# Place columns turned in the second graph layer, seven gathered pairs in flight there, inputs on two queues, and a reordered start

## The chip, the cores and the metric

The kernel runs on one core of one Trainium2 chip. The metric is the device time of one execution in microseconds (us), the median of several runs. PE is the matrix engine, DVE the vector engine, ACT the scalar engine, POOL the GpSimd engine and SP the engine that here only issues DMAs.

## The reference

Two graph layers on 6250 nodes of 128 numbers and 106250 edges, sorted by their destination `dst`:

```python
h = relu(layernorm(x))
x = x + L0(h, src, dst, edge_type)          # attention over 4 edge types
h = relu(layernorm(x))
x = x + L1(h, edge_attr, src, dst)          # two-layer network on every edge, and on every node

# L0, for each of the 4 relations, 8 heads of 16 numbers
xr = h @ W;  logit = leaky_relu(es[src] + ed[dst], 0.2)      # es, ed: xr with a_src, a_dst
alpha = softmax of logit over the edges of one dst and one type
out = segment_sum(alpha * xr[src], dst) + b
# then the 4 outputs (gelu, @ W_cross) and h @ W_self are weighed by a softmax over these 5

# L1: an edge (s, d) is used in both directions
edge_in = [nf[src_full], nf[dst_full], ef_full]              # 128 + 128 + 64
msg = leaky_relu(edge_in @ We1) @ We2
red = segment_sum(msg, dst_full)
return leaky_relu([nf, red] @ Wn1) @ Wn2
```

## The kernel before

**Tiles.** Nodes are cut into NU = 50 tiles of 126, each into two blocks of 63 (NBK = 100 blocks). Since edges are sorted by destination, a block's edges are one stretch of at most 9 × 128 = 1152 edges (TB = 9 tiles, CAP edges), whose first edge is read from a small table on the chip (`st0`) at run time. An edge that doesn't belong to the block is masked by `inb`.

**Start (L190–L433).** SP loads `src`, `dst`, `et`; ACT's queue issues the loads of x in ten-tile blocks (L220, L222), then the weights and the attention vectors (L230–L241). DVE works out where blocks start, and SP writes and reloads `e2`, the edges' source rows and destinations, by block (`ct`, L347: 100 DMAs). The table loop (L353–L378) runs over the 50 tiles: every ten tiles the layernorm and relu of ten (`layernorm_relu`, L145–L152: sums on DVE, the Square L148 on ACT), then for each tile a transpose L358, matmuls L365, the copy L366 into `row`, an own row with x and the bias `blb` (L373, stored by ACT L374) and two stores of `row` to the table `xt` on POOL's queue (L377). Behind the loop, ten groups of `ct` are turned from rows into columns (L384–L393: a cast, two transposes, a copy into `xi`, a subtraction into `dloc`), and `srci`, `inb` and `key` are worked out from these (L395–L402).

**Layer 0 (L438–L859).** NS = 25 steps of four blocks (Q = 4), nine tiles each. POOL's gathers (L81, from `xt` by `xi`) run LA0 = 17 tiles ahead in a ring of 18 tiles `xg`. The edge work of step s + 1 is woven by the written order into step s: `masks`, `logits` (L521), the scans of `soft` (L552–L570), which make the softmax, `turn` (L577), then in step s + 1 itself `messages` (L584, L591, L592); `nodes` of the step before (L621–L705) is handed out in pieces within `messages`, and ends with stores to `abtab`, layer 1's table. `loads(s)` (L498 and around) brings sixteen DMAs of lane data on SP's queue. For the second layer, DVE counts how many edges have their source in each of the 50 tiles (`count`, L721, in steps 0 to 3 by the written order), ranks them (`rank`, L763–L766), and writes every edge's place to `plcd`. In steps 20 to 24 `place_load` (L774–L778) reads these places back by block, ten DMAs a group into one of three buffers `ctp`, and `place_turn` (L781–L789) turns them into columns `placei`: one transpose, three DVE operations.

**Layer 1 (L914–L1076).** 450 pairs of tiles. `gather_pair(n + 3)` (two L81 gathers from `abtab` into one of five buffers `ag`), matmuls L1046, the sum L1048, the leaky relu L1049 and L1050, the source column L1051 into `s` (four buffers), two scatters L1054 of s by `placei` into `m2d`, and the sums over the destination L1064. `ready(u + 1)` (L987–L1021) prepares the next tile: loads of `fe`, `db` and rows of `abtab` on SP, transposes L1013. `windows(j)` (L935–L966) sums the scattered rows by source, once the scatters of one of five parts are issued: loads `mt` on SP (L943), L959, the one-hot L963, matmuls L964. `node_update` (L872–L908) ends the kernel together with the last part's windows.

**What sets the order.** Every engine runs its instructions in one order, which a scheduler makes from the program's order, the data's ties and the buffers. An instruction passed to `keep_in_program_order` isn't moved against its neighbours. DMAs are issued by the engine named, in that engine's order; POOL issues all gathers and scatters.

Of the kernel before, what the change touches and what calls it, by code (L numbers as in the profile page):

```python
# [21 lines left out]
P = 128  # L22
# [4 lines left out]
R = 4  # L27
# [29 lines left out]
LA0 = 17  # L57
NCS = 4
# [18 lines left out]
AHEAD = 3  # L77
# [8 lines left out]
def kernel(ctx: ExitStack, tc: tile.TileContext, x, src, dst, ef, et, w_rel, a_src, a_dst,  # L86
# [106 lines left out]
    with ExitStack() as prep:  # L193
# [4 lines left out]

        ints = {}
# [13 lines left out]
        for u0 in range(0, NU, 10):  # L213
            nc.gpsimd.memset(x_sb[:, u0:u0 + 10, :], 0.0)
            for q in range(2):
                n0 = u0 * DB + q * GB
                k = 10 if u0 + 10 < NU else 9
                xq = x[u0 * DB:(u0 + k) * DB, :].rearrange("(u q r) c -> q r u c", q=2, r=GB)[q]
                for r0, r1 in ((0, 48), (48, GB)):
                    nc.scalar.dma_start(x_sb[q * 64 + r0:q * 64 + r1, u0:u0 + k, :], xq[r0:r1])  # L220
        for h, n in halves(NU - 1):
            nc.scalar.dma_start(x_sb[h, NU - 1, :], x[n, :])  # L222


        wall = cpool.tile([P, R * XR + R * H + C + 2 * H], F32, name="wall")
        wx = wall[:, 0:R * XR].rearrange("p (r c) -> p r c", r=R)
        wd = wall[:, R * XR:R * XR + R * H].rearrange("p (r h) -> p r h", r=R)
        wso = wall[:, R * XR + R * H:]
        wr = cpool.tile([P, R, C], F32, name="wr")
        nc.scalar.dma_start(wr, w_rel.rearrange("r i o -> i r o"))  # L230
        nc.scalar.dma_start(wso[:, 0:C], w_self)
        nc.scalar.dma_start(wcx[:, 0:C], w_cross)
        nc.scalar.dma_start(brT, b_rel.rearrange("r c -> c r"))
        blb = cpool.tile([P, C], F32, name="blb")
        nc.scalar.dma_start(blb, b_l.partition_broadcast(P))
        tmp = cpool.tile([P, R * C], F32, name="tmp")

        def scores(o, w, a, r):

            ab = wpool.tile([P, R * C], F32, name="ab")  # L240
            nc.scalar.dma_start(ab[:, 0:r * C], a.partition_broadcast(P))  # L241
            tt(tmp[:, 0:r * C].rearrange("p (r c) -> p r c", r=r), w,
               ab[:, 0:r * C].rearrange("p (r c) -> p r c", r=r), op=ALU.mult)
            red(o, tmp[:, 0:r * C].rearrange("p (r h d) -> p r h d", r=r, d=D), axis=AX.X, op=ALU.add)

        nc.gpsimd.tensor_copy(wx[:, :, 0:C], wr)
        scores(wx[:, :, C:XR], wr, a_src.rearrange("r h d -> (r h d)"), R)
        scores(wd, wr, a_dst.rearrange("r h d -> (r h d)"), R)
        ws1 = wso[:, 0:C].rearrange("p (r c) -> p r c", r=1)
        scores(wso[:, C:C + H].unsqueeze(1), ws1, a_src_l.rearrange("h d -> (h d)"), 1)  # L250
        scores(wso[:, C + H:C + 2 * H].unsqueeze(1), ws1, a_dst_l.rearrange("h d -> (h d)"), 1)
        wc1 = wcx[:, 0:C].rearrange("p (r c) -> p r c", r=1)
        scores(wcx[:, C:C + H].unsqueeze(1), wc1, a_src_l.rearrange("h d -> (h d)"), 1)
# [97 lines left out]

        for u in range(NU):
            if u % 10 == 0:  # L353
# [9 lines left out]
            w = R * XR // 2  # L363
            for k in range(2):
                nc.tensor.matmul(ps[:, k, 0:w], hT, wall[:, k * w:(k + 1) * w], start=True, stop=True)  # L365
            nc.vector.tensor_copy(row.rearrange("p (a c) -> p a c", a=2), ps[:, :, 0:w])  # L366
# [12 lines left out]


        first = cpool.tile([P, NBK, TB], F32, name="first")
        nc.gpsimd.iota(first, [[GB, NBK], [0, TB]], base=0, channel_multiplier=0, allow_small_or_imprecise_dtypes=True)
        w = CG * TB
        for g in range(NBK // CG):  # L384
            ct = cts[g]
            ctf = wpool.tile([w, 2, P], F32, name="ctf")
            nc.vector.tensor_copy(ctf, ct)
            tp = pp.tile([P, 2, w], F32, name="tp")
            for a in range(2):
                nc.tensor.transpose(tp[:, a, :], ctf[:, a, :], ident[0:w, 0:w])  # L390
            s = slice(g * w, (g + 1) * w)
            nc.vector.tensor_copy(xi[:, s], tp[:, 0, :])
            tt(dloc[:, s], tp[:, 1, :], first.rearrange("p b i -> p (b i)")[:, s], op=ALU.subtract)  # L393
        ti = cpool.tile([P, NT], I32, name="ti")
        ts_(ti, xi, R - 1, None, op0=ALU.bitwise_and)  # L395
        ts_(srci, xi, 2, None, op0=ALU.logical_shift_right)
        nc.vector.tensor_copy(srcf, srci)
        ts_(inb, dloc, 0.0, None, op0=ALU.is_ge)
        stt(inb, dloc, float(GB), inb, op0=ALU.is_lt, op1=ALU.mult)
        stt(key, ti, 64.0, dloc, op0=ALU.mult, op1=ALU.add)  # L400
        stt(key, key, 1.0, inb, op0=ALU.add, op1=ALU.mult)
        ts_(key, key, -1.0, None, op0=ALU.add)  # L402
# [35 lines left out]
    with ExitStack() as s1_:  # L438
# [38 lines left out]
        xgs, lanes, pes = {}, {}, {}  # L477

# [142 lines left out]
        def nodes(s, g, gt, last):  # L621
# [20 lines left out]
            tt(va, gt[:, :, 0:R].rearrange("p v t -> p t v"), gt[:, :, 1:R + 1].rearrange("p v t -> p t v"), op=ALU.is_gt)  # L642
# [64 lines left out]
        def node_turns(s, done):  # L707

            if done:
                yield from nodes(s - 1, *done, s == NS)  # L710
            yield
            g = (s - NS) * 3 + NBK // CG
            for k in range(3):
                if 0 <= g + k < NBK // CG:
                    place_turn(g + k)
                    yield

        def count(b):

            ind = wp.tile([P, J], U8, name="ind", bufs=1)  # L720
            ts_(ind, skey, float(b), None, op0=ALU.is_equal, op1=ALU.add, accum_out=cnt[:, b:b + 1])  # L721
# [38 lines left out]
        def rank(b):  # L760
# [7 lines left out]

        trash = cp.tile([P, CG * TB], F32, name="trash")
        nc.gpsimd.iota(trash, [[0, 2], [P, CG * TB // 2]], base=E, channel_multiplier=1,  # L770
                       allow_small_or_imprecise_dtypes=True)
        pcs = {}

        def place_load(g):  # L774
            ct = wp.tile([CG * TB, P], F32, name="ctp", bufs=3)
            regs = first_of(st0, g * CG, CG, E - CAP)
            for k in range(CG):
                nc.sync.dma_start(ct[k * TB:(k + 1) * TB], plcd[0, ds(regs[k], CAP)].rearrange("(i p) -> i p", p=P))  # L778
            pcs[g] = ct

        def place_turn(g):  # L781
            w = CG * TB
            s = slice(g * w, (g + 1) * w)
            tp = pa.tile([P, 512], F32, name="ent")
            nc.tensor.transpose(tp[:, 0:w], pcs.pop(g), ident[0:w, 0:w])
            pf = wp.tile([P, w], F32, name="pf", bufs=1)
            tt(pf, tp[:, 0:w], trash, op=ALU.subtract)
            tt(pf, pf, inb[:, s], op=ALU.mult)
            tt(placei[:, s], pf, trash, op=ALU.add)  # L789

# [8 lines left out]

        masks(0)  # L800
# [11 lines left out]
        for s in range(NS):  # L812
# [7 lines left out]
            for i in range(TB):  # L820
# [15 lines left out]
                if s < NCS:  # L836
                    for b in range(s * TB + i, NU, NCS * TB):
                        count(b)
# [8 lines left out]
                g = (s - NS + 1) * 3 + NBK // CG + (i - 3) // 2  # L847
                if 0 <= g < NBK // CG and i in (3, 5, 7):
                    place_load(g)
# [812 lines left out]
```

## Time and profile before

| what | value |
|---|---|
| runs shown | 4169.11, 4176.27, 4177.46 us; median 4176.27 |
| the profiled execution | 4172.47 us, span of the instructions 4170.7 us |
| granted PE clock | 0.86 (mean) |
| busy | PE 3111.7, DVE 2830.8, POOL 2899.4, ACT 1574.8 us |
| memory traffic | 754.26 MB, 180 GB/s |
| POOL's first store of a row to `xt` | 60.73 us |
| POOL's first gather in layer 0 | 164.16 us |
| POOL's first instruction of layer 1 | 1556.43 us |

The page's second part shows the span in 40 slices of 104 us, a digit for the tenths that an engine was busy. Its DMA row and GB/s row are those of the transfers:

```profile
DVE  6767899999777744455556665566657666577755
ACT  2356666656666532222222332222222222222211
DMA  6645444445555417666578886788868888588754
GB/s 180 168 102 120 113 113 114 114 112 119 118 119 122 105 41 202 175 180 184 165 212 247 252 253 197 227 249 240 246 197 265 242 237 251 170 263 274 242 164 139
```

Slices 1 and 2 are the start, 2 to 14 are layer 0, slice 15 with its 41 GB/s is the passage to layer 1, slices 16 to 38 are layer 1, and the last two the end. The busy time of an indirect DMA on POOL is the time in which its descriptors are made; the transfer itself runs behind it on the DMA engines. A group's idle time that ends by "issue" waited for nothing that the profile shows.

### The profile page before, as it was taken

Reading aid. Unit: us, or ns where it says so; the run is one execution under the profiler, and the core shown is the slowest. Engines: PE = TensorE matmul, PEld = TensorE weight load, DVE = VectorE, ACT = ScalarE, POOL = GpSimd, SP = SyncE. Lnnn points to the kernel's source line nnn. Section 1 sums busy time; section 2 is a strip of 40 time slices with the busy share of each in tenths; the row PEclk is TensorE's granted clock in tenths of the full one; section 3 lists DMA queues with packets and bytes.
Section 4 is the critical chain, followed back from the end, with each engine's and each line's share of the span. In section 5 each row is a group of like instructions: output and inputs, shape, how many; then the busy total and the mean of one; then the engine's idle time right before and its main releaser. Section 6 shows DMA issues by size and latency. Waiting matters only on the chain. (4 is left out here: it accounts for less than half of the span.)

```text
span 4170.7 us, 43560 instructions
## 1 busy us (share of the span) xinstructions
PE 3111.7 (75%) x11258; PEld 1790.3 (43%) x11258; DVE 2830.8 (68%) x5244; ACT 1574.8 (38%) x2994; POOL 2899.4 (70%) x2887
## 2 busy tenths in 40 slices
PE   4558877777888855666678887688768787688888
PEld 3346555555666642222234443344324333244456
DVE  6767899999777744455556665566657666577755
ACT  2356666656666532222222332222222222222211
POOL 5777777777777506777777777777777777777700
PEclk9768878888888868788889898888989989899999
DMA  6645444445555417666578886788868888588754
GB/s 180 168 102 120 113 113 114 114 112 119 118 119 122 105 41 202 175 180 184 165 212 247 252 253 197 227 249 240 246 197 265 242 237 251 170 263 274 242 164 139
DMA packets 414703, 754.26 MB, mean 181 GB/s; under 512 B 182863, under 2 KB 249525, under 8 KB 414445
## 3 DMA queue, kind: packets, MB, share of 16 engines
q0 software_dynamic: 148800, 430.91, 35.6%
q1 hardware_dynamic: 230376, 288.41, 26.6%
q10 hardware_dynamic: 35268, 32.07, 2.7%
q8 instruction: 92, 1.51, 0.2%
q14 instruction: 167, 1.36, 0.1%
HBM read 586.43 MB, written 164.69 MB: 180 GB/s over the span
## 5 line engine op out<-in xcount | busy, mean ns | idle before, releaser
L81 POOL DMA_INDIRECT xg<-xt,xi x900 | 980.5, 1089 | 289.0 <-issue 237.8
L81 POOL DMA_INDIRECT ag<-abtab,srci x900 | 907.4, 1008 | 303.4 <-issue 203.0
L1054 POOL DMA_INDIRECT m2d<-s,placei x900 | 913.9, 1015 | 288.6 <-issue 213.7
L1046 PE MATMUL z<-rhs,lt 128*128 128x512 f32 x1800 | 1037.5, 703 | 0.6 <-ACT lt L1017 0.6
L1050 DVE TENSOR_TENSOR s<-s,z 128x1024 f32<-128x1024 f32 x450 | 548.3, 1220 | 560.9 <-ACT z L1049 559.1
L1064 PE MATMUL sums<-s,oh 128*64 128x256 f32 x1800 | 338.3, 459 | 486.5 <-DVE s L1050 485.5
L1048 DVE TENSOR_TENSOR s<-z,ag 128x1024 f32<-128x1024 f32 x450 | 549.5, 1221 | 189.5 <-PE z L1046 156.0
L1049 ACT ACTIVATE z<-s 128x1024 f32<-128x1024 f32 x450 | 461.0, 1024 | 389.1 <-DVE s L1048 388.6
L592 PE MATMUL acc<-oh,msg 128*128 128x256 f32 x1800 | 501.9, 421 | 71.1 <-DVE oh L591 51.4
L1046 PEld LDWEIGHTS z<-rhs,lt 128*128 128x128 f32 x1800 | 353.2, 216 | 449.3 <-issue 442.8
L1051 ACT COPY s<-srcf 128x2 f32<-128x2 f32 x450 | 86.9, 193 | 1207.4 <-DMA m2d<-s,placei 1193.4
L964 PE MATMUL sums<-mt,ohw 128*128 128x256 f32 x2024 | 528.1, 394 | 9.2 <-DVE ohw L963 9.2
L964 PEld LDWEIGHTS sums<-mt,ohw 128*128 128x128 f32 x2024 | 392.4, 200 | 202.8 <-issue 133.9
L592 PEld LDWEIGHTS acc<-oh,msg 128*128 128x128 f32 x1800 | 363.3, 212 | 164.3 <-DVE oh L591 74.0
L1064 PEld LDWEIGHTS sums<-s,oh 128*64 128x64 f32 x1800 | 98.8, 149 | 729.7 <-DVE s L1050 570.5
L591 DVE TENSOR_SCALAR oh<-iota,key 128x256 f32<-128x256 f32 x900 | 309.6, 365 | 93.0 <-PE acc L592 88.7
L599 ACT ACTIVATE junk<-dt,nthr 128x1152 bf16<-128x1152 f32 x250 | 313.8, 1255 | 17.2 <-DMA dt<-dtyp 12.3
L963 DVE TENSOR_SCALAR ohw<-col,at 128x128 f32<-128x128 f32 x1012 | 250.5, 299 | 19.5 <-PE sums L964 11.3
L584 DVE TENSOR_TENSOR msg<-xg,pt 128x512 f32<-128x512 f32 x225 | 148.6, 676 | 86.5 <-PE pt L577 81.3
L1013 PE MATMUL tp<-ident,fe 128*128 128x128 f32 x450 | 86.6, 299 | 138.1 <-ACT lt L1017 107.2
L1017 ACT COPY lt<-tp 64x384 f32<-64x384 f32 x300 | 141.7, 472 | 111.3 <-PE tp L1013 62.7
L1013 PEld LDWEIGHTS tp<-ident,fe 128*128 128x128 f32 x450 | 58.9, 151 | 212.3 <-ACT lt L1017 140.8
(276 smaller groups left out, 3467.0 us busy)
## 6 DMA issues: line engine op xcount, KB each, us to landing
mt<-m2d SPq DMA_DIRECT2D x156, 514.0 KB
db<-in_dst_dram SPq DMA_DIRECT2D x200, 288.0 KB
mt<-m2d SPq DMA_DIRECT2D x53, 642.5 KB
dt<-dtyp SPq DMA_DIRECT2D x100, 288.0 KB
fe<-in_edge_attr_dram SPq DMA_DIRECT2D x100, 288.0 KB
mt<-m2d SPq DMA_DIRECT2D x41, 385.5 KB
xg<-xt,xi POOLq DMA_INDIRECT x900
ag<-abtab,srci POOLq DMA_INDIRECT x900
```

What stands on the lines that cost most here:

```text
L81: nc.gpsimd.indirect_dma_start(out=o, out_offset=None, in_=table, in_offset=bass.IndirectOffsetOnAxis(ap=idx.bitcast(I32), axis=0))
L591: ts_(oh.rearrange("p t n -> p (t n)"), iota, key[:, k:k + 1], None, op0=ALU.is_equal)
L592: nc.tensor.matmul(acc[q // 2][:, :, q % 2, :], msg[:, q, :], oh, start=(i == 0 and q % 2 == 0), stop=(i == TB - 1), skip_group_check=True)
L599: nc.scalar.activation(junk, lanes[s]["dt"][v], AF.Sign, bias=nthr[:, u, t:t + 1], accum_out=g[:, v, t:t + 1])
L963: ts_(oh, col, at[:, i:i + 1], None, op0=ALU.is_equal)
L964: nc.tensor.matmul(sums, oh, mt[:, i, 0:HID], start=(i == 0), stop=(i == n - 1))
L1046: nc.tensor.matmul(z[:, q, :], lt[q][:, i * P:(i + 1) * P], rhs[(2 * u + q) % 4], start=True, stop=True)
L1048: tt(s[:, :, 0:2 * HID], z, ags.pop(n), op=ALU.add)
L1049: nc.scalar.mul(z, s[:, :, 0:2 * HID], 0.01)
L1050: tt(s[:, :, 0:2 * HID], s[:, :, 0:2 * HID], z, op=ALU.max)
L1054: st = nc.gpsimd.indirect_dma_start(out=m2d, out_offset=bass.IndirectOffsetOnAxis(ap=placei[:, k:k + 1], axis=0), in_=s[:, q, HID:HID + MW ...
L1064: nc.tensor.matmul(sums[q * 64:(q + 1) * 64, :], oh[:, q * TB + i, :], s[:, q, 0:HID], start=(i == 0), stop=(i == TB - 1))
```

## The change

1. `AHEAD` becomes 7: a pair is gathered seven pairs ahead, and `ag` has nine buffers in place of five.
2. `place_load` and `place_turn` leave layer 0. A generator `places` in layer 1 does the same for one group: ten loads into a single buffer `ctp`, and the turn in the bank of PSUM that `ready` uses. Group 0 is done before the first tile, groups 1 to 9 in tiles 2, 7, ..., 42: loads at the tile's second pair, the turn at its last.
3. The weights, attention vectors (each into a buffer of its own, `ab0` to `ab3`, read once) and `blb` are loaded at the head of ACT's queue; of x, only the first two blocks stay there, the others and the last tile go to SP's queue.
4. The columns are turned in the last ten passes of the table loop, a group in each (`columns`), instead of behind it; the integer and key work L395–L402 goes into layer 0's opening, with `ti` in the memory of `key`.
5. 28 counts (`NC0`) stand ahead of the first step's masks, and the other 22 one per tile of the steps 0 to 2, pinned to the program's order, as is one operation `va` of `nodes` (L642).

The built kernel has, in its order on each engine, 18 DMAs on ACT's queue ahead of the first Square (29 before), ten place loads on SP ahead of the first `fe`, and 18 gathers on POOL (ten before) ahead of the first wait for an L1048.

```diff
+NC0 = 28
...
-AHEAD = 3
+AHEAD = 7
...
+        nc.scalar.dma_start(wr, w_rel.rearrange("r i o -> i r o"))
+        nc.scalar.dma_start(wso[:, 0:C], w_self)
+        nc.scalar.dma_start(wcx[:, 0:C], w_cross)
+        atts = []
+        for a in (a_src.rearrange("r h d -> (r h d)"), a_dst.rearrange("r h d -> (r h d)"),
+                  a_src_l.rearrange("h d -> (h d)"), a_dst_l.rearrange("h d -> (h d)")):
+            ab = cpool.tile([P, a.shape[0]], F32, name=f"ab{len(atts)}")
+            nc.scalar.dma_start(ab, a.partition_broadcast(P))
+            atts.append(ab)
+        blb = cpool.tile([P, C], F32, name="blb")
+        nc.scalar.dma_start(blb, b_l.partition_broadcast(P))
...
-                    nc.scalar.dma_start(x_sb[q * 64 + r0:q * 64 + r1, u0:u0 + k, :], xq[r0:r1])
+                    (nc.scalar if u0 < 20 else nc.sync).dma_start(x_sb[q * 64 + r0:q * 64 + r1, u0:u0 + k, :], xq[r0:r1])
         for h, n in halves(NU - 1):
-            nc.scalar.dma_start(x_sb[h, NU - 1, :], x[n, :])
+            nc.sync.dma_start(x_sb[h, NU - 1, :], x[n, :])
...
+        def columns(g):
+            ct = cts[g]
+            ctf = wpool.tile([w, 2, P], F32, name="ctf")
+            nc.vector.tensor_copy(ctf, ct)
+            tp = pp.tile([P, 2, w], F32, name="tp")
+            for a in range(2):
+                nc.tensor.transpose(tp[:, a, :], ctf[:, a, :], ident[0:w, 0:w])
+            s = slice(g * w, (g + 1) * w)
+            nc.vector.tensor_copy(xi[:, s], tp[:, 0, :])
+            tt(dloc[:, s], tp[:, 1, :], first.rearrange("p b i -> p (b i)")[:, s], op=ALU.subtract)
...
         for u in range(NU):
+            if u >= NU - NBK // CG:
+                columns(u - NU + NBK // CG)
...
+        ti = key.bitcast(I32)
+        ts_(ti, xi, R - 1, None, op0=ALU.bitwise_and)
+        ts_(srci, xi, 2, None, op0=ALU.logical_shift_right)
+        nc.vector.tensor_copy(srcf, srci)
+        ts_(inb, dloc, 0.0, None, op0=ALU.is_ge)
+        stt(inb, dloc, float(GB), inb, op0=ALU.is_lt, op1=ALU.mult)
+        stt(key, ti, 64.0, dloc, op0=ALU.mult, op1=ALU.add)
+        stt(key, key, 1.0, inb, op0=ALU.add, op1=ALU.mult)
+        ts_(key, key, -1.0, None, op0=ALU.add)
...
+            tc.keep_in_program_order(c)
...
+        for b in range(NC0):
+            count(b)
         masks(0)
...
                 if s < NCS:
-                    for b in range(s * TB + i, NU, NCS * TB):
-                        count(b)
+                    b = NC0 + s * TB + i
+                    if b < NU:
+                        count(b, True)
...
-                g = (s - NS + 1) * 3 + NBK // CG + (i - 3) // 2
-                if 0 <= g < NBK // CG and i in (3, 5, 7):
-                    place_load(g)
...
+        def places(pool, bank, g):
+
+            w = CG * TB
+            s = slice(g * w, (g + 1) * w)
+            ct = pool.tile([w, P], F32, name="ctp", bufs=1)
+            regs = first_of(st0, g * CG, CG, E - CAP)
+            for k in range(CG):
+                nc.sync.dma_start(ct[k * TB:(k + 1) * TB], plcd[0, ds(regs[k], CAP)].rearrange("(i p) -> i p", p=P))
+            yield
+            tp = bank()[:, 0:w]
+            nc.tensor.transpose(tp, ct, ident[0:w, 0:w])
+            pf = pool.tile([P, w], F32, name="pf", bufs=1)
+            tt(pf, tp, trash, op=ALU.subtract)
+            tt(pf, pf, inb[:, s], op=ALU.mult)
+            tt(placei[:, s], pf, trash, op=ALU.add)
...
+            for _ in places(wp, bank, 0):
+                pass
             for _ in ready(0):
                 pass
...
+                more = u % 5 == 2 and 2 * u + 6 < NBK
+                plcs = places(wp, bank, (2 * u + 6) // CG) if more else iter(())
...
+                    if i in (1, TB - 1):
+                        next(plcs, None)
```

## The prediction, made before the changed kernel was run

> **What bounds the kernel now.** First the page's busy shares and its 40 slices, then the groups by line, then the waits of POOL, last the timeline around POOL's idle stretches. Columns of the groups: count, busy us in all, mean ns, idle just before them and what ended most of it; of the waits: us in all, times, longest; of the timeline: start, duration, instruction, and in brackets its wait.
> ```profile
> POOL 5777777777777506777777777777777777777700
> L81 POOL DMA_INDIRECT xg<-xt,xi x900 | 980.5, 1089 | 289.0 <-issue 237.8
> L81 POOL DMA_INDIRECT ag<-abtab,srci x900 | 907.4, 1008 | 303.4 <-issue 203.0
> L1054 POOL DMA_INDIRECT m2d<-s,placei x900 | 913.9, 1015 | 288.6 <-issue 213.7
> ```
> POOL is level at 7 in every slice of both layers, and its idle time before indirect DMAs ends mostly by "issue": it waits for nobody. Layer 0 is 900 gathers from 164.16 to about 1433 (1.41 each), layer 1 is 1800 DMAs from 1556 to 3967 (1.34 each). What the change can win lies where POOL stands still: the start (to 164), the gap between the layers, and the waits within layer 1.
> ```profile
> POOL iota L919 <- DMA abtab<-at: 123.1, 1, 123.1
> POOL iota L445 <- DVE key L400: 8.2, 1, 8.2
> POOL ag L81 <- DVE s L1048: 42.8, 50, 14.1
> POOL m2d L1054 <- DVE s L1050: 18.4, 34, 2.4
> ```
> The gap is 123.1 us; the start ends with 8.2 on the keys; the 84 waits in layer 1 come to 61.2, of which 84 × 0.30 = 25 is the gap that every issue has, and 13.8 the first fill: about 22 to 25 us are real.
>
> **A. Start of the table loop.** POOL's stores of xt set the loop's pace (77.8 busy of the 95 us from 60 to 155), so an earlier first tile moves all.
> ```profile
> 26.11 1.48 DVE L147 TENSOR_TENSOR h_sb<-x_sb,ln_st 128x1280 f32<-128x1280 f32 x1
> 10.56 30.17 ACTq L220 DMA_DIRECT2D x_sb<-in_x_dram  x16
> 47.86 1.27 ACT L148 ACTIVATE sq<-h_sb 128x1280 f32<-128x1280 f32 x1
> 54.92 1.48 DVE L152 SCALAR_TENSOR_TENSOR h_sb<-h_sb,ln_st 128x1280 f32<-128x1280 f32 x1
> ```
> The Square's operand is done at 27.59; it runs at 47.86, behind the 29 DMAs that ACT issues to 46.56. The first h_sb is done at 56.40, 8.54 after the Square starts. Changed, 18 DMAs precede the Square. By shares: 8 x loads at 30.17/16 = 1.89 is 15.1, ten small ones at 0.45 is 4.5, from 8.3: 28, then a table load of 1.28: Square from 29, h_sb at 38 (−18). By the mean of all 29 ((46.56 − 8.26)/29 = 1.32, 18 × 1.32 = 24): Square at 33.6, h_sb at 42.2 (−14). Weights now land beside the first x blocks, so I go a little below the second: **−13** [−20.3, the whole wait 47.86 − 27.59, to 0]. The store of own needs blb, which landed at 48.9; it is now the eighth DMA on the queue, so it can't take the wait over.
>
> The DMA engines' share was 1.12 and 0.85 from 10 to 30 us, 0.65 and 0.49 from 30 to 50: by these rows the wait is one of ACT's instruction order, not of DMA bandwidth.
>
> The Trainium skill, "DMA: Bandwidth & Descriptors", section "Issuing engines are not separate DMA queues", speaks against this part: DMAs issued from several engines share the same 16 engines, and only the sequencers' time is saved. By that rule alone the loads of x on a second queue bring nothing and the sum would be about 13 smaller in size, −19; the rule says nothing of a compute instruction that stands behind the issues, which is what the row at 47.86 shows.
>
> **B. End of the loop to the first gather.**
> ```profile
> 152.42 1.16 POOL L377 DMA_DIRECT2D xt<-row  x2 [1.29 <-DVE row L366]
> 161.72 0.35 POOL L445 IOTA iota<- 128x256 f32 x1 [8.15 <-DVE key L400]
> 164.16 1.05 POOL L81 DMA_INDIRECT xg<-xt,xi  x1 [0.25 <-issue]
> ```
> The last store is issued at 153.58; ten column groups and the keys lie behind it, and POOL waits 8.15. Now each group (cast, two transposes, copy, subtract; DVE's share 0.29 + about 0.6) lies in one of the last ten passes, where DVE is 60 of 100 busy and POOL sets the pace; the keys go behind the pool's opening beside gathers. Removed: **−7** [−8.15 to 0, if the pool's opening still waits for another DVE instruction]. Added: columns in ten passes, **+3** [0 to 10 × 0.5 = +5, half of DVE's part showing]; keys beside gathers, **+2** [0 to +4]: DVE operations with two SBUF inputs stretch a POOL DMA from 0.95 to 1.2–1.35 (L556 1.35, L654 1.23), and there are six instructions of about 1 us. A to B: −15.
>
> **Counts.** All 50 ran from 166.6 to 221.3 (1.07 each) ahead of the first scan. With 28 ahead and 22 pinned into steps 0 to 2 the scan can come up to 22 × 1.07 = 23.5 us earlier. POOL doesn't wait there: its ring of 18 tiles is never empty of buffers before 1433. **0**; in the steps 7 or 8 counts each are covered by DVE's 29 idle of 100 us (300 to 400). Without this cover: +23.5.
>
> **C. End of layer 0.**
> ```profile
> 1423.72 11.78 SPq L778 DMA_DIRECT2D ctp<-plcd  x20
> 1436.74 0.52 SPq L498 DMA_DIRECT2D db<-in_dst_dram  x1
> 1463.60 0.33 PE L521 MATMUL lg<-ne,pen 16*128 16x384 bf16 x1
> 1483.15 2.56 DVE L552 TENSOR_TENSOR_SCAN f<-km,l 128x1152 f32<-128x1152 f32 x1 [0.62 <-ACT l L534]
> 1504.07 2.13 PE L577 MATMUL pt<-sel,l 128*128 128x32 f32 x9 [0.28 <-ACT l L569]
> ```
> L577 starts once a step. The seven gaps before the last are 46.6 to 49.9 (mean 48.5), the last is 72.8 (1431.3 to 1504.1). Three ctp buffers make SP hold place loads until older ones are turned; the 16 loads of step 24's lanes stand behind them on SP (to 1455.6), so logits, scan and turn of step 24 come one after another behind step 23, not interleaved. With the place loads gone SP has nothing in front, and in the built order step 24's logits lie within step 23 as in any step: −24.3. Three of the ten turns (each transpose plus three DVE operations) leave the tail too, but nodes(23) now ends behind the last messages: +3. **−21** [−24.3 to 0, if something else, such as the gathers' landing, holds step 24].
>
> **D. First fill of layer 1.** fe was issued at 1556.39, the first L1048 came at 1582.90, and POOL stood 14.07 after ten gathers (resumed at 1584.40). Changed, SP issues ten place loads first (11.78/20 = 0.59 each, +5.9); POOL does 18 gathers, 8 × 1.26 = 10.1 us more of work that waits for nothing. Its resumption lies 5.9 later at worst, and 10 us more work stands done, but that is only moved: the gathers are 900 in all, and POOL's stand at the first scatter is what counts. **+1** [−4.5 if the fill hides fe's way, +5.6 if all SP time shows].
>
> **E. Seven ahead.**
> ```profile
> 1740.20 0.19 ACT L1051 COPY s<-srcf 128x2 f32<-128x2 f32 x1 [6.01 <-DMA m2d<-s,placei]
> 1745.79 1.23 DVE L1048 TENSOR_TENSOR s<-z,ag 128x1024 f32<-128x1024 f32 x1 [3.22 <-PE z L1046]
> 1747.29 0.99 POOL L81 DMA_INDIRECT ag<-abtab,srci  x1 [2.20 <-DVE s L1048]
> ```
> A gather into a buffer waits for the L1048 that read it; with five buffers gather n+5 stands right before scatter n and waits for L1048 of pair n, with nine gather n+9 does the same. s keeps four buffers, and the row of L1051 shows that chain: it waits for the scatter four pairs back. So the wait that shows is between L1048 and the scatter of one pair, which the count of ag buffers doesn't touch: **−2** [−25, all of the real waits, to 0].
>
> **F. Places in layer 1.** Nine groups of ten SP loads and one turn each. DVE 9 × 3 × 0.28 = 7.5 us and PE 3 us, spread over 2400 us in which DVE idles a third: covered. On SP each burst takes 5.9 to 7.2 us (0.59 to 0.72 per issue: 40 took 28.82), and seven of the nine lie among the window loads:
> ```profile
> DVE at L959 <- DMA mt<-m2d: 84.7, 45, 14.5
> ```
> These waits of DVE (of 2050 to 3960) hardly reach POOL now (its later waits are at most 2.4). **+3** [0 to 7 × 7.2 = +50].
>
> **G. Last pairs.** Without gathers, the last nine pairs (before: five) run scatters alone, where the chain z, L1048, L1049, L1050 is longer than two scatters; the excess was about 7 us for five: **+2** [0 to +6].
>
> **Sum.** −13 −7 +3 +2 −21 +1 −2 +3 +2 = −32 on a span of 4170.7: 4138.7, and the run's 4172.47 becomes 4140. The median shown, 4176.27, lies 3.8 above that run: 4144.
>
> **Rivals.** (1) Depth does help: what POOL waits for at L81 is the burst of other DVE work (L963, ready's masks), and nine buffers let it run ahead: all 25 of E, 4144 − 23 = 4121, .14. For: 50 waits name L1048; against: the relation above. (2) The start doesn't move: x is held by DMA (share 1.12 and .85 to 30 us) and the loop by POOL; A gives 0, nearly +15 with B: 4159, .12. (3) The end of layer 0 stays: step 24 then waits for its last gathers (landed by about 1436) and for DVE: +21, 4165, .08. (4) Slower: the window loads stand on SP behind the place bursts, which wait for ctp's single buffer and 0.6 to 0.7 per issue; the windows come late and bunch on DVE and PE in front of L1048, and POOL waits. Full price 7 × 7.2 = +50: 4194. It decides from (32 + 8.4)/7 = 5.8 us per burst reaching POOL; for it: 84.7 us of waits on mt already; against: those are absorbed now. .11.
>
> **How the numbers follow.** My sum .55; its own range is 4126 to 4162, from −18 to +18: A, C and F each off by about 10 together. The range of 8 in 10 takes rival 1 with 9 more (4112) below, rivals 2 and 3 above and stops short of 4194: 4112 to 4170. 0.2%, about what a measurement of this kernel tells from no change, is 8.4 us: faster is below 4167.9. Faster: .53 + .14 + .10 + .05 = .82; same: .02 + .02 + .03 + .03 = .10; slower: .08, from rival 4.
>
> **What would show it.** A: first xt store near 47 instead of 60.73, Square not behind x loads. B: first gather about 149, no wait on key before it. C: the last gap of L577 near 48.5 and POOL's wait on abtab near 100. D: the first wait on L1048 within 6 us of 14. E: waits of POOL at L81 and L1054 still about 60 in all. F: waits at L959 up by less than 60, POOL's unchanged. Wrong would be: a start unchanged, a gap still above 115, or layer 1 longer than 2430 (now 2411) from its first gather to its last scatter.

## The result, and the profile after

Ten runs each on the chip of the first times: 4149.05 us (4143.98 to 4167.52) against 4173.16 (4164.88 to 4181.6), ratio 0.9945, 95% interval 0.9931 to 0.996: 23 us faster by the ratio and 24 by the medians, where 32 had been forecast. The profiled run has a span of 4142.2 us, 28.5 below that of before. All stage times below come from these two executions; line numbers are those of the changed kernel (L82 is L81 of before, L1059 is L1048, L586 is L577, L352 is L347).

The page: POOL's slices, and its three groups (count, busy us, mean ns, idle before them).
```profile
POOL 6777777787777616777777777777777777777600
L82 POOL DMA_INDIRECT xg<-xt,xi x900 | 985.8, 1095 | 289.3 <-issue 240.3
L1065 POOL DMA_INDIRECT m2d<-s,placei x900 | 915.7, 1017 | 297.8 <-issue 212.4
L82 POOL DMA_INDIRECT ag<-abtab,srci x900 | 905.5, 1006 | 293.7 <-issue 209.2
```
POOL is busy at the same level in both layers as before; the lone 0 between the layers (slice 15 before) has become a 1. The waits of POOL, and one of DVE, over the whole span of the changed kernel:
```profile
POOL iota L902 <- DMA abtab<-at: 98.6, 1, 98.6
POOL iota L443 <- PE po L390: 8.6, 1, 8.6
POOL ag L82 <- DVE s L1059: 32.7, 46, 7.3
POOL m2d L1065 <- DVE s L1061: 26.8, 30, 2.9
DVE at L963 <- DMA mt<-m2d: 120.0, 68, 14.9
```
The same of the kernel before, where the view ahead of the prediction stops at 3960 us, some 10 us short of layer 1's end:
```profile
POOL m2d L1054 <- DVE s L1050: 23.4, 37, 2.8
DVE at L959 <- DMA mt<-m2d: 104.4, 61, 14.5
```
The passage fell from 123.1 to 98.6. At the start the 8.2 on a key is gone, but an 8.6 on PE stands in its place. In layer 1 the two waits come to 59.5, before 66.2 (42.8 and 23.4). The difference is the first fill, whose wait fell from 14.1 to 7.3; layer 1 as a whole is no shorter for it, as the table shows. DVE's wait for window loads rose by 15.6, and no wait of POOL shows it.

Stage by stage, from POOL's first and last instructions of each:

| stage | before | after | difference | forecast |
|---|---|---|---|---|
| start of the span to the first gather | 164.16 | 155.04 | −9.1 | −15 |
| layer 0's gathers | 1269.2 | 1274.4 | +5.2 | 0 |
| last gather to layer 1's first instruction | 123.1 | 98.6 | −24.5 | −21 |
| layer 1, to the end of the last scatter | 2413.8 | 2413.5 | −0.3 | +4 |
| the end | 200.5 | 200.7 | +0.2 | 0 |

The rows sum to −28.5. The start is the stage that missed its forecast most. Its timeline in the changed kernel (start, duration, instruction, wait):
```profile
24.46 1.28 ACT L149 ACT_TABLE_LOAD   x1 [24.46 <-DMA x_sb<-in_x_dram]
32.84 1.48 DVE L148 TENSOR_TENSOR h_sb<-x_sb,ln_st 128x1280 f32<-128x1280 f32 x1
34.35 1.27 ACT L149 ACTIVATE sq<-h_sb 128x1280 f32<-128x1280 f32 x1 [8.61 <-DVE h_sb L148]
45.28 1.32 POOL L399 DMA_DIRECT2D xt<-row  x2 [17.62 <-DVE row L388]
...
19.84 12.14 SPq L246 DMA_DIRECT2D x_sb<-in_x_dram  x12
62.79 81.27 SPq L352 DMA_DIRECT2D ct<-e  x100
...
145.62 0.29 DVE L363 CAST ctf<-ct 90x256 f32<-90x256 int32 x1 [5.99 <-DMA abtab<-zr]
146.32 0.42 PE L380 MATMUL tp<-ident,h_sb 128*128 128x128 f32 x1
149.99 0.35 POOL L443 IOTA iota<- 128x256 f32 x1 [8.56 <-PE po L390]
155.04 1.14 POOL L82 DMA_INDIRECT xg<-xt,xi  x1 [0.72 <-issue]
```
In the kernel before, the loads of `ct` were these:
```profile
36.64 81.37 SPq L347 DMA_DIRECT2D ct<-e  x100
```
The head moved by as much as was forecast: ACT's queue is through at 24.46, the Square runs at 34.35 and waits for DVE, no longer for the queue; the first xt store is 15.4 earlier (60.73 to 45.28). But SP now issues the later loads of x first, and its 100 small loads of `ct` run from 62.79 to 144.06, where before they ran from 36.64 to 118.01. The last column group needs the last `ct`: its cast is at 145.62 (the profile names the store behind it on SP; the time fits the end of `ct`), and the last table pass, L380, stands behind it on PE. So POOL waits 8.56 at the end of the loop.

Lines of the step that ends layer 0, in the changed kernel:
```profile
1406.27 0.49 SPq L509 DMA_DIRECT2D dt<-dtyp  x1
1438.20 0.33 PE L530 MATMUL lg<-ne,pen 16*128 16x384 bf16 x1
1452.42 2.55 DVE L561 TENSOR_TENSOR_SCAN f<-km,l 128x1152 f32<-128x1152 f32 x1
1471.65 3.62 PE L586 MATMUL pt<-sel,l 128*128 128x32 f32 x16 [4.67 <-ACT l L578]
1528.04 0.20 POOL L902 IOTA iota<- 128x64 f32 x1 [98.62 <-DMA abtab<-at]
```
Step 24's lane loads are on SP some 30 us before its logits start, and those begin at 1438.20 within step 23. The last gap of L586 is 47.9, like the seven before it (47.1 to 48.2).

### The profile page after: what moved, and what is told of

Its sections match the earlier page's. It is cut to its first block, busy times and chain, and to the rows that moved or that the text cites. A ratio compares the mean times of both kernels' runs of the same rounds, so it can differ in the third digit from the quotient of the medians.

```text
span 4142.2 us, 43508 instructions
## 1 busy us (share of the span) xinstructions
PE 3141.5 (76%) x11258; PEld 1793.5 (43%) x11258; DVE 2821.2 (68%) x5244; ACT 1590.2 (38%) x3000; POOL 2907.1 (70%) x2887
## 5 line engine op out<-in xcount | busy, mean ns | idle before, releaser
L82 POOL DMA_INDIRECT xg<-xt,xi x900 | 985.8, 1095 | 289.3 <-issue 240.3
L82 POOL DMA_INDIRECT ag<-abtab,srci x900 | 905.5, 1006 | 293.7 <-issue 209.2
L1059 DVE TENSOR_TENSOR s<-z,ag 128x1024 f32<-128x1024 f32 x450 | 549.8, 1222 | 203.1 <-PE z L1057 165.5
L601 PE MATMUL acc<-oh,msg 128*128 128x256 f32 x1800 | 523.0, 432 | 69.6 <-DVE oh L600 43.1
L608 ACT ACTIVATE junk<-dt,nthr 128x1152 bf16<-128x1152 f32 x250 | 314.0, 1256 | 38.4 <-DMA dt<-dtyp 34.6
```

The lines of the kernel that those rows point to most:

```text
L82: nc.gpsimd.indirect_dma_start(out=o, out_offset=None, in_=table, in_offset=bass.IndirectOffsetOnAxis(ap=idx.bitcast(I32), axis=0))
L601: nc.tensor.matmul(acc[q // 2][:, :, q % 2, :], msg[:, q, :], oh, start=(i == 0 and q % 2 == 0), stop=(i == TB - 1), skip_group_check=True)
L608: nc.scalar.activation(junk, lanes[s]["dt"][v], AF.Sign, bias=nthr[:, u, t:t + 1], accum_out=g[:, v, t:t + 1])
L1059: tt(s[:, :, 0:2 * HID], z, ags.pop(n), op=ALU.add)
```

## The experiments

The twelve ran on three other chips, four on each: experiments one to four, five to eight, nine to twelve. On all three every kernel takes some 800 us longer: the kernel before 4970, 4965 and 4972, the changed one, which ran on the second of them only, 4945. A ratio is to the kernel before on the same chip; where stages of two chips stand side by side it is said. A view of one late step of layer 0, in which the instruction order is the same, shows what is different there. Columns of this view by stretches: stretch and its length, busy us of PE, PE's weight loads, DVE, ACT and POOL (with counts), granted clock, DMA share, GB/s. First the changed kernel on the chip of the result, then as experiment five:
```profile
1281.00:1328.00 47.00, 42.13 (x173) 30.10 (x172) 35.76 (x82) 33.02 (x60) 36.03 (x37) 0.81 0.55 128
```
```profile
1858.00:1933.00 75.00, 47.63 (x173) 32.01 (x173) 35.66 (x82) 32.67 (x59) 34.78 (x36) 0.73 0.32 76
```
The same work takes 75 us in place of 47, PE at a lower clock, the other engines with the same busy time and more idle; POOL's gathers in layer 0 now wait for ACT (160.5 us on L608 alone in experiment five). Layer 1 takes 2713 to 2746 in place of 2413. The start up to some 160 us and the last 200 us are the same. A ratio there is good to 0.3 to 0.4%, some 15 to 20 us, so parts worth 5 to 25 us are read from their stage and not from the whole time. A stage scatters too: the first gather came at 152.86 to 155.77 in the six of these experiments (one, two, four, five, eight, ten) whose start is written as in the changed kernel.

**One, eight, two and three: the depth, the buffers s, and a third queue for x.** In one and eight, the same kernel in two groups:
```diff
-AHEAD = 7
+AHEAD = 3
```


> The changed kernel with AHEAD back at 3 (five buffers ag); all else stays. My theory: seven ahead brought nothing, since gather n + bufs still stands right before scatter n and waits for L1059 of pair n in both. Then layer 1, from POOL's first instruction of it to its last scatter, stays at 2413.5 us within 5, POOL's wait 'ag on L1059' is 33 to 43 us as in both kernels, and the time is that of the changed kernel, 4149, within 5. Rival: the depth did help and paid for the place loads that came into layer 1 (F, up to 50): then this kernel is 15 to 25 slower, near 4170, and layer 1 is 2430 or more.

> AHEAD back at 3 in the changed kernel, as in the first group (where its layer 1 took 2722 us, that with eight s buffers 2724, the one with AHEAD 7 and x on POOL 2713, the one with places in layer 0 2731). Theory: nothing changes, layer 1 within 5 of the changed kernel's of this group, time within 4. Rival: seven ahead is worth 8 to 25 us where the chip's DMA is quick, layer 1 2425 or more.

Measured: the ratio to the kernel before was 0.9966 (0.9938 to 0.9995) and, in the second group, 0.9995 (0.9959 to 1.0031); the changed kernel beside the latter 0.9967 (0.9937 to 0.9996). By whole times that is unclear. Layer 1 took 2722.4 and, beside the changed kernel's 2727.8 on the same chip, 2721.0: the depth brings layer 1 nothing there, and the −0.3 of the result says the same of depth and place loads together. POOL's waits in the second group, first with seven ahead, then with three:
```profile
POOL ag L82 <- DVE s L1059: 129.3, 39, 7.9
```
```profile
POOL ag L82 <- DVE s L1059: 144.5, 48, 14.6
```
The longest of them, 14.6, is the first fill, which the deeper ring shortens; behind the fill the same waits come to 121.3 and 129.9.

```diff
-AHEAD = 7
+AHEAD = 3
...
-                    s = wp.tile([P, 2, 2 * HID + 1], F32, name="s", bufs=4)
+                    s = wp.tile([P, 2, 2 * HID + 1], F32, name="s", bufs=8)
```


> The changed kernel with AHEAD 3 and eight buffers s in place of four: the memory of four ag buffers is given to s. Theory: what makes POOL wait in layer 1 is that DVE and ACT can be only four buffers s ahead of the scatters, so a burst of other DVE work (L967, the masks of the next tile) reaches POOL; with eight they run further ahead. POOL's waits on L1059 and L1061 beyond 0.30 each, about 35 us now, fall below 15, layer 1 falls from 2413 to 2385 to 2400 and the time to 4125 to 4138. Rival: the wait is between L1059 and the scatter of one pair, which no number of buffers changes, or DVE never gets ahead: layer 1 stays within 5 of 2413 and the time near 4149.

Measured: layer 1 2724.2, with four buffers on the same chip 2722.4; ratio 0.9967 (0.9935 to 0.9999). My theory fell: four more buffers of s change nothing either. On these chips more of neither ring makes layer 1 shorter; on the chip of the result it wasn't tried.

```diff
-                    (nc.scalar if u0 < 20 else nc.sync).dma_start(x_sb[q * 64 + r0:q * 64 + r1, u0:u0 + k, :], xq[r0:r1])
+                    (nc.scalar if u0 < 20 else nc.gpsimd).dma_start(x_sb[q * 64 + r0:q * 64 + r1, u0:u0 + k, :], xq[r0:r1])
...
-            nc.sync.dma_start(x_sb[h, NU - 1, :], x[n, :])
+            nc.gpsimd.dma_start(x_sb[h, NU - 1, :], x[n, :])
```


> The changed kernel with the fourteen later loads of x issued by POOL, which stands idle then, in place of SP. Theory: the start gained 9 and not 15 because on SP these loads push the 100 ct loads from 36.64 to 62.79, so the last columns come at 145.6, the last table pass stands behind them on PE and POOL waits 8.6. Here the ct loads start near 37 to 45 and end by 126; no wait of 8 us at the end of the loop; first gather at 145 to 149 in place of 155.04, time 4139 to 4143. Rival: the last passes are held by their own work (PE, DVE, the own stores), whatever the queue of x: first gather stays within 2 of 155, time near 4149. It could also lose at the head, if the loads push POOL's iotas (bl, node) back: then ct starts later than 45 and the first xt store later than 48.

Measured: the miss that the last sentence named. POOL's iotas, from which DVE finds the block starts, slid behind the loads (`bl` at 26.92, in the changed kernel at 10.65), `ct` started at 63.65, the first xt store came at 64.54 and the first gather at 163.79, 9.5 later than in experiment one on the same chip, whose start is written as in the changed kernel (154.31). The ratio 0.9907 (0.9879 to 0.9935) is nevertheless better, by layer 0, of which more below.

**Four and eleven: the places.** Places back in layer 0 of the changed kernel, with the old `place_load`, `place_turn` and three ctp buffers:
```diff
+                g = (s - NS + 1) * 3 + NBK // CG + (i - 3) // 2
+                if 0 <= g < NBK // CG and i in (3, 5, 7):
+                    place_load(g)
...
-            for _ in places(wp, bank, 0):
-                pass
...
-                    if i in (1, TB - 1):
-                        next(plcs, None)
```

> The changed kernel with place loads and turns back in steps 20 to 24 of layer 0, with three ctp buffers, as before; all else stays. Theory: the passage to layer 1 fell from 123.1 to 98.6 because step 24's lane loads no longer stand behind place loads on SP. Here the last gap of L586 is again about 70 and not 48, POOL's wait on abtab 118 to 125, layer 1 about the same (2409 to 2414), time 4165 to 4175. Rival: the passage fell for another reason (the order of the last steps without turns in nodes, the pinned operation): wait on abtab stays near 99 to 105 and the time near 4149 to 4155.

And the reverse, the kernel before with the places alone in layer 1 (the same lines with the signs turned, `AHEAD = 3`, the old start and counts):

> The kernel before with the places moved into layer 1 alone (AHEAD stays 3, start and counts as before). Theory: this one part is worth 20 to 25 of the change's 24: the passage from the last gather of layer 0 to POOL's first instruction of layer 1 is 97 to 100 where the kernel before has 123 (118 to 120 and 143 on the chip of the earlier groups), layer 1 within 6 of that of the kernel before, ratio to before 0.994 to 0.997. Rival: without seven ahead the place loads reach POOL in layer 1 (up to 50), and the ratio is 0.998 or above.

POOL's waits between the layers: places in layer 0; the changed kernel; the kernel before with only the places moved. These are three chips; experiment one, on the chip of the first of them, has 118.6.
```profile
POOL iota L933 <- DMA abtab<-at: 143.5, 1, 143.5
```
```profile
POOL iota L902 <- DMA abtab<-at: 118.9, 1, 118.9
```
```profile
POOL iota L888 <- DMA abtab<-at: 119.6, 1, 119.6
```
The passage is 20 longer than on the chip of the result, but on one chip the places make a difference of 24.9 (143.5 against 118.6), and the one edit, made alone, brings the short passage. Both edits move loads and turns together; that it is the loads is read from SP's queue, with places in layer 0:
```profile
1907.64 12.05 SPq L789 DMA_DIRECT2D ctp<-plcd  x20
1920.93 0.53 SPq L507 DMA_DIRECT2D db<-in_dst_dram  x1
...
1947.35 0.49 PE L530 MATMUL lg<-ne,pen 16*128 16x384 bf16 x1
```
The 20 place loads stand right ahead of step 24's lane loads, and its logits start at 1947, behind step 23's turn at 1913.3; the last gap of L586 is 74.6, in all the others, which have no places in layer 0, it is 47 to 49. Ratios: 0.994 (0.9907 to 0.9972) with the places in layer 0, 0.9958 (0.9933 to 0.9983) for the places alone. So by whole times experiment four speaks for its rival: the longer passage doesn't show in them, and the medians of experiments four, one and two on that chip, 4954.64, 4952.88 and 4955.1, are the same. Its layer 0 was 1736.5, where one and two had 1749.0 and 1756.6, which takes back 12 to 20 of the 24.9. Layer 1 of the places alone took 2729.4, with AHEAD 3: place loads don't need the deeper ring.

**Five: the changed kernel itself.**

> The changed kernel itself once more, as the measure for the others of this group, since the first group met a chip on which every kernel, that of before too, took some 800 us longer. Theory: on a chip like that of the result, ratio to before 0.993 to 0.996, passage from last gather of layer 0 to POOL's first instruction of layer 1 98 to 99, layer 1 2408 to 2419 (last scatter minus that instruction), first gather at 154 to 156. Rival: the terms of 5 us in the ledger of one execution (layer 0 +5.2) are of that execution alone: layer 0's gathers then take 1266 to 1272 in this one.

Measured: first gather at 153.72, passage 118.9, layer 1 2727.8, ratio 0.9967 (0.9937 to 0.9996). The chip was not one like that of the result, so whether layer 0's +5.2 belongs to the one execution stays open.

**Six, seven, nine and twelve: the start.** First, x's later loads on ACT, in the table loop at tiles 2, 8 and 16, pinned there:
```diff
-                    (nc.scalar if u0 < 20 else nc.sync).dma_start(x_sb[q * 64 + r0:q * 64 + r1, u0:u0 + k, :], xq[r0:r1])
...
+                    c = nc.scalar.dma_start(x_sb[q * 64 + r0:q * 64 + r1, u0:u0 + k, :], xq[r0:r1])
...
+            if u in (2, 8, 16):
+                x_in({2: 20, 8: 30, 16: 40}[u], True)
```


> The changed kernel with the fourteen later loads of x issued by ACT in the table loop (pinned at tiles 2, 8 and 16), none on SP. Theory: on SP these loads push the 100 ct loads back from 36.6 to 62.8, and the last columns and the last table pass wait for them. Here ct starts at 36 to 45 and ends by 126, POOL waits less than 3 for PE po or columns behind its last stores, the last xt store is issued by 143, first gather at 146 to 150 in place of 155, and the kernel is 5 to 9 us faster than the changed one of this group. Rival: the last passes are slow by their own work, or x now comes late for tiles 20 on: the last xt store stays at 148 to 152, first gather within 2 of 155.

A miss, ratio 0.997 (0.9936 to 1.0005). `ct` ran from 40.70 to 119.48 as expected, but the table loop slowed: last xt store at 171.09, first gather at 175.27. ACT's waits in that kernel:
```profile
ACT edbd L404 <- DMA x_sb<-in_x_dram: 12.1, 2, 8.2
ACT hT L394 <- DMA ct<-e: 8.7, 3, 4.4
```
ACT's copies, on which each table pass hangs, waited 20.8 us in these two rows, about as much as the first gather is later (21.6 than in experiment five). The profile names DMAs, though neither copy reads x or `ct`; the 12.1 stand right behind the loads of x that ACT issues in the loop. The loads themselves also came later: the last operation of the layernorm of tiles 20 to 29 ran at 85.3 in place of 62.8. Which of the two took more isn't told apart.

Columns behind the loop again, x as in the changed kernel:
```diff
-            if u >= NU - NBK // CG:
-                columns(u - NU + NBK // CG)
...
+        for g in range(NBK // CG):
+            columns(g)
```


> The changed kernel with the columns turned behind the table loop again; loads of x as in the changed kernel. Theory: the table passes don't wait for ct any more: the last xt store is issued by 143 (150.6 now), while the last columns still wait for ct to 145.6, and POOL's opening of layer 0 waits for them: first gather at 151 to 155, time within 4 of the changed kernel, so that turning the columns inside the loop bought nothing here. Rival: columns in the loop bought the 7 us of the prediction: first gather at 159 or later and 5 us slower.

Measured: last xt store 143.46 (149.41 in experiment five on the same chip), POOL's wait 4.6 on the last column, first gather 151.08 against 153.72. Ratio 0.9976 (0.9944 to 1.0007). With the columns inside the loop the last table passes stand behind `ct`, and the last xt store is 5 to 6 later. At the first gather 1.8 to 2.6 of this is left (152.91 in experiment eight, which has the changed kernel's start on this chip), no more than the first gather scatters: turning the columns inside the loop won nothing here, and that it cost something isn't shown.

All of x on ACT's queue, weights still ahead:
```diff
-                    (nc.scalar if u0 < 20 else nc.sync).dma_start(x_sb[q * 64 + r0:q * 64 + r1, u0:u0 + k, :], xq[r0:r1])
+                    nc.scalar.dma_start(x_sb[q * 64 + r0:q * 64 + r1, u0:u0 + k, :], xq[r0:r1])
...
-            nc.sync.dma_start(x_sb[h, NU - 1, :], x[n, :])
+            nc.scalar.dma_start(x_sb[h, NU - 1, :], x[n, :])
```


> The changed kernel with all loads of x on ACT's queue (weights still at its head), none on SP: the split of x alone is undone. Theory: the first Square stands behind all 22 loads of x again, at 40 to 52 in place of 34, and the first xt store comes at 52 to 64 in place of 45; but ct starts by 45 and ends by 128, so POOL doesn't wait for the last columns, and the first gather is at 155 to 162: the split gains 15 at the head and gives back 6 to 10 at the loop's end. Rival: putting the weights first made the head early, and the split did nothing (all DMAs share the same engines): first xt store within 2 of 45, first gather at 145 to 149.

```profile
50.33 1.27 ACT L149 ACTIVATE sq<-h_sb 128x1280 f32<-128x1280 f32 x1
41.22 78.59 SPq L352 DMA_DIRECT2D ct<-e  x100
159.65 1.04 POOL L82 DMA_INDIRECT xg<-xt,xi  x1 [1.66 <-issue]
```
Experiment ten, on the same chip, has the changed kernel's start: Square 34.02, first xt store 44.95 where it is 61.38 here (−16.4), `ct`'s end 143.61 where it is 119.8, first gather 154.24 where it is 159.65. The split gains 16.4 at the head, and 5.4 of it are left at the first gather. The ratio of this kernel was 0.9923 (0.9896 to 0.995).

Columns behind the loop, and x's loads on SP spread among those of `ct`:
```diff
+            if u0 < 30:
+                x_in(u0, nc.scalar if u0 < 20 else nc.sync)
...
             cts.append(ct)
+            if g in (1, 3):
+                x_in(30 if g == 1 else 40, nc.sync, True)
...
-            if u >= NU - NBK // CG:
-                columns(u - NU + NBK // CG)
...
+        for g in range(NBK // CG):
+            columns(g)
```


> The changed kernel with the columns behind the table loop, and the loads of x on SP spread: tiles 20 to 29 ahead, 30 to 39 after the second group of ct, 40 to 49 after the fourth. Theory: ct starts at 42 to 52 and ends at 128 to 138 in place of 143, the last xt store is issued by 143, columns end right behind it, and the first gather is at 145 to 149 (155.04 in the changed kernel, 151.08 with the columns alone behind the loop): 4 to 9 us faster than the changed kernel, a version that beats both. Rival: the table passes are then held by the same SP queue, x of tiles 30 or 40 coming late: last xt store after 146, first gather 151 or later.

```profile
42.00 14.71 SPq L362 DMA_DIRECT2D ct<-e  x20
56.76 4.07 SPq L246 DMA_DIRECT2D x_sb<-in_x_dram  x4
62.65 19.45 SPq L362 DMA_DIRECT2D ct<-e  x20
82.15 2.61 SPq L246 DMA_DIRECT2D x_sb<-in_x_dram  x4
92.01 48.33 SPq L362 DMA_DIRECT2D ct<-e  x60
147.33 1.83 POOL L82 DMA_INDIRECT xg<-xt,xi  x1 [0.84 <-issue]
```
`ct` begins 20 us earlier and ends at 140.33, two later than expected; the first gather is at 147.33, 6.9 before that of experiment ten on the same chip. Ratio 0.9889 (0.9851 to 0.9927): faster than the kernel before by 55 us, and the changed kernel had 0.9967 (0.9937 to 0.9996) on another of these chips. Only the 6.9 us at the first gather are shown to be this stage's (5.5 to 8.4 against all six starts as in the changed kernel); whether it beats the changed kernel side by side, there or on a chip like that of the result, wasn't run.

**Ten: all 50 counts ahead.**
```diff
-NC0 = 28
+NC0 = 50
```

> The changed kernel with all 50 counts ahead of the first step's masks (22 of them moved back from the steps 0 to 2). Theory: the first turn L586 comes up to 23 later (22 x 1.07), and where POOL sets layer 0's pace (step of 48 us) nothing comes of it. On a chip where a step takes 72 to 75 and POOL waits for ACT and DVE, 5 to 20 of it reach the end of layer 0; there the time rises by up to 0.4%. Rival: the counts in the steps cost as much as they cost ahead (they stretch POOL's gathers beside them), time and end of layer 0 unchanged or earlier.

Measured: ratio 0.9871 (0.983 to 0.9912), the lowest of all; layer 0 1694.0. The theory fell: the first turn came at 282, with 28 counts ahead at 278 to 281 (one, two, four, five and eight, other chips). Whether 50 ahead are faster than 28 on one chip wasn't run. In the changed kernel on the chip of the result the room of the moved counts shows as a wait:
```profile
211.59 2.56 DVE L561 TENSOR_TENSOR_SCAN f<-km,l 128x1152 f32<-128x1152 f32 x1 [23.00 <-ACT l L543]
```
The 23.5 us of 22 counts became 23.0 of waiting for the logits, which need the gathers of nine tiles: the first scan starts 56.6 us after the first gather, before it was 57.7.

**What layer 0 does on these chips.** Its length differs between kernels in which nothing written of it differs, on one chip: 1721.8 (three) against 1749.0 and 1756.6 (one, two), and 1721.4 (six) against 1765.0, 1753.2 and 1762.9 (five, seven, eight). The order built need not be the same: compared with the changed kernel, DVE's and PE's orders differ within steps 0 to 15 in the ninth and tenth experiment, 0 to 14 in the twelfth, and are identical from there on. In steps 5 to 8 the gaps of L586 were 85, 77, 75 and 52 in the fifth, 60, 60, 52 and 69 in the sixth on the same chip; from step 16 on all kernels are at 71 to 78. In the traces, DVE and ACT have the changed kernel's order through layer 0 in the first, second, fifth and eighth, whose layer 0 took 1749.0 to 1765.0 on two chips; in the other seven made from the changed kernel the order differs in some of these steps, and layer 0 took 1694.0 to 1736.5 in six of them and 1753.2 in the seventh experiment. So a small edit of the start can reorder sixteen steps of layer 0 and weigh more there than by itself; that it is the order which does it goes with these times and isn't shown by an experiment of its own. Why a step is sometimes 55 and sometimes 75 is not settled.

## Why the prediction was right, and where not

- **A** (−13, bounds −20.3 to 0) held: −15.4 at the first store, −13.5 at the Square, which no longer stands behind loads of x; the ninth experiment beside the tenth shows that the split is what does it, not the weights' place. That the size came so near is luck. The sum set all 18 DMAs behind 8.3 us and had the queue free at 28 to 32; eight of them were issued ahead of the first load of x at 7.42, and it was free at 24.46. What then held the Square was its operand, done at 34.32 where before it was done at 27.59: DVE, which now begins with the attention scores at 7.44, worked without a pause up to it. The sum has no term for DVE. Against that stood the Trainium skill, "DMA: Bandwidth & Descriptors", section "Issuing engines are not separate DMA queues": what a second queue saves is the sequencer's time. These runs agree with the sentence and not with the −19 drawn from it: ACT's issues lasted to 46.56 before, to 49.03 in the ninth experiment and to 24.46 in the changed kernel, and a compute instruction stood behind them.
- **B** (−7 +3 +2) is the step that failed. It forecast a first gather at 149, and it came at 155.04. The prediction priced the columns in the loop by DVE's half and POOL's pace, and has no term for the arrival of `ct`, whose loads had been issued by 118 before, 34 us ahead of the loop's last store. It counted the loads of x that left ACT's queue and not the queue that they came to: 14 loads on SP, ahead of the stores and the 100 loads of `ct`, moved these by 26 us, past the last columns; and the columns' new place put the last table pass behind them. By the table B was −9.1 + 15.4 = +6.3 in place of −2. The twelfth experiment, which spreads these loads and takes the columns out of the loop, wins 6.9 back. The +2 for the keys beside gathers isn't seen: they ran from 146.9 to 155.3, beside the last stores and POOL's opening, and the first 36 gathers took 46.0 us, before 47.1.
- **Counts** (0) held, but for a reason that the prediction doesn't name: the scan that it put up to 23.5 us earlier came only 1.1 sooner after the first gather, since it waited 23.0 for the logits.
- **C** (−21) held: −24.5 in the result and 24.9 between two kernels on another chip, with SP's queue as forecast. It is most of the −28.5. In whole times the eleventh experiment agrees (0.9958 for this part alone), while the fourth doesn't show it.
- **D, E, F, G** (+4 together) came to −0.3. Depth and place loads together left layer 1 as long as it was: neither rival 1 nor rival 4 came. The first fill's wait on L1048 fell to 7.3, a little more than D allowed, and DVE's 15.6 us more waiting for windows shows in no wait of POOL. Single terms can't be told apart at this size.
- **Layer 0's +5.2** against 0 is the other half of the miss: from −32 to −28.5 the start lost 5.9 and layer 0 5.2, the passage gave 3.5 more and layer 1 4.3, and the end lost 0.2. Its cause is open. Counted from the first gather, the changed kernel's 216th gather, at 443 us, is 0.7 behind that of before, and its 324th, at 611 us, 6.7. The counts had ended at 355, the keys at the first gather; what differs in this stretch is the order of DVE's instructions. That the order in these steps changes with edits elsewhere is all the other chips show of it.
- The median moved by 24 and not by the 28.5 of the profiled pair; run to run both kernels scatter by 17 to 24 us.

## What to carry to other kernels

When DMA issues leave one queue, price them on the queue they come to, by what stands behind them there and when that is needed: fourteen loads moved away from ACT won 15 us at the head and put SP's `ct` back by 26, and 9 were left at the first gather. Work "hidden" in a loop's last passes puts those passes behind whatever that work waits for. A set of loads that holds a queue on its buffers at the end of a phase can be worth moving, even into a phase that is already full: its 24.5 us were most of what was won here. A deeper gather ring shortened the first fill's wait by 7 and no stage. And a forecast whose number comes true can have two errors that cancel, as the Square's did: ask of each wait that goes what the next one is.

## What the runs showed of the hardware

One program, with the same instruction order, took 4149 us on one chip and 4945 on another (and the kernel before 4173 and, on three others, 4965 to 4972), the difference being in the two long stages and the passage between them: a layer-0 step 47 and 75 us, layer 1 2413 and 2728, at a granted TensorE clock of 0.855 and 0.801 over the run, while the start and the end took the same time on both. What makes these chips differ isn't shown. Two readings of a stage came out alike on both (the places' part of the passage, 24.5 and 24.9; the first gather, 155.0 and 153.7), while the ratio of whole times, 0.9945 (0.9931 to 0.996) and 0.9967 (0.9937 to 0.9996), doesn't say which stage it comes from.
